# A four-layer convolution network on one NeuronCore: image b's depthwise taps in layer 3 move from TensorE to VectorE, and the order of taps, pieces and copies follows two clocks

## The chip, the cores and the metric

The program runs on one core of one Trainium2 chip. The metric is the device time of one execution in microseconds (us), the median of the runs shown. A separate profiled execution gives the span and the trace. Engines are named as in the profile: PE is TensorE's matmuls, PEld its weight loads, DVE is VectorE, ACT is ScalarE, POOL is GpSimd, SP is SyncE.

## The reference, cut to what matters

The input is x of shape (4, 48, 256, 256) in fp32. Each of four layers computes x + f(group_norm(x)). Layers 1 and 2 are recurrent scans over rows and columns and are not touched here. Layers 0 and 3 are gated depthwise networks:

```python
# layer 3 (HIDDEN = 144, C2 = 288); layer 0 is the same in another order with 96 / 192
y = einsum('oc,bchw->bohw', w_in, x)                 # 48 -> 288 channels
f = rfft2(y in 8x8 patches) * fft_mask; y = irfft2(f)
y = depthwise_conv3x3(y, w_dw)                       # 9 taps a channel
x1, x2 = split(y, 2, axis=1)
out = einsum('oc,bchw->bohw', w_out, gelu(x1) * x2)  # 144 -> 48
```

## The kernel before, in words

Layer 3 works on pairs of images, called a and b, and on strips of 8 rows: 2 pairs with 32 strips each and one short last step a pair (`tail`), so 64 full steps and 2 short ones. In a step 128 of the 144 channels of each half of each image fill one tile: `z_a0`, `z_a1`, `z_b0`, `z_b1` (half 0 feeds the Gelu, half 1 multiplies it). The last 16 channels of both halves and both images share the tile `z_m`. A step consists of these pieces, with the lines of the kernel before:

- `normed` (L904): four ACT instructions scale the raw strip into `u`. `turned` (L916): PE transposes `u`, ACT copies it to `xt`. `waves` (L930): PE transforms `xt`, ACT copies to `xf`.
- `spectrum` (L941): per column block q two PE matmuls into a PSUM tile `pz` and two DVE multiplications with the mask into `z`. Sixteen a step, two to a piece.
- `pixels` (L961): for each of the five groups 16 PE matmuls into `pp` and two ACT copies into `z_a0` and so on, after a copy of the two halo rows (by POOL for a and b, by ACT for m).
- `taps` (L988): the depthwise convolution on PE. A tap is a 32x32 diagonal matrix times a shifted window of 512 elements. Two generators, `lane(0)` and `lane(1)` (L1051), each own two of the four blocks of 32 channels; one turn of a lane issues one tap of one group, 8 matmuls. In a step each lane takes nine turns for each half of image a, then of b, and one of the two lanes nine for m. The results are held in PSUM tiles `pd`.
- `gate` (L1001): ACT takes the Gelu of half 0's `pd`, DVE multiplies it with half 1's into `g_a`, `g_b` or `g_m`.
- `mixed` (L1011): 40 PE matmuls of 32 rows by 64 columns into two PSUM tiles `po`, then eight DVE additions of the raw rows (`xo`) and the DMAs out on SP's queue.

All PSUM tiles of layer 3 come from one pool of four (L825[...])[...].

What sets the order: the whole program is unrolled while it is built. `in_turns` (L482) is the planner. In each round every lane takes one turn, which earns `pace` credit; pieces from the list `work` (L1070) are issued in their fixed order while the credit lasts or when no lane moved, if their condition (`free`, `full`) holds. Each piece carries a cost in the planner's us. Layer 0 has the same planner and similar pieces, for 64 strips. There the last 32 channels of both halves and images, `rests`, are already convolved on DVE by `unit` (L297), whose taps (L313) are handed out by `aside` (L515) according to a balance `ahead`; the main channels are convolved on PE (L278), and `mixed` (L340), `turned` (L367), `waves` (L381) and `back` (L399) follow. In layer 0 the program orders of PE and DVE are the order of issue (`manual_schedule`, L156); in layer 3 only PE's is (L826), and DVE, ACT, POOL and the queues are ordered by the framework. [...]

## Time and profile before

| | us |
|---|---|
| median of 3 runs (lowest, highest) | 14483.5 (14481.45, 14491.1) |
| the profiled execution, its own time | 14477.21 |
| its span in the profile | 14475.4 |
| PE busy in the span | 13474.0 |
| DVE busy | 5981.7 |
| ACT busy | 3295.6 |
| layer 0, from its first taps on PE to its last (264.72 to about 3230) | about 2965 |
| layer 3, from its first transposes to the end (9095.56 to 14475.4) | 5380 |

The span begins with some 230 us of statistics of the input, then comes layer 0, then layers 1 and 2 (to about 9090), then layer 3. A busy share is the time in which at least one instruction of the engine ran. fp32 matmuls appear twice in the records, so a tap's 8 matmuls are 16 records. The mean duration of one record does not say how fast records follow each other[...]; where a duration is needed, the distance from start to start in the timeline is the better one. One step of layer 3 is seen between two stores: the `xo` additions began at 9711.71 and, two steps later, at 9877.41, so a step took 82.9 us there.

### The profile page before, as it was taken

The numbers are of one execution on the slowest core, as the hardware profiler recorded it, in microseconds if no ns is written. First come the engines' busy times: TensorE is split into PE (matmuls) and PEld (weight loads), VectorE is DVE, ScalarE is ACT, GpSimd is POOL, SyncE is SP. The second block draws the span as 40 slices with busy tenths as digits, with TensorE's granted clock in tenths as the row PEclk, the third lists the DMA queues.
The fourth block names the chain that finished last, engine by engine and source line by source line (L and its number), as shares of the span: only waits on it lengthen the run. The fifth ranks groups of instructions, "written<-read, shape, count | busy, mean of one in ns | idle before, by whom it ended". The sixth has DMA issues, their size and how long they took to land.

```text
span 14475.4 us, 377862 instructions
## 1 busy us (share of the span) xinstructions
PE 13474.0 (93%) x175216; PEld 8571.1 (59%) x175216; DVE 5981.7 (41%) x10946; ACT 3295.6 (23%) x3108; POOL 1496.9 (10%) x1228
## 2 busy tenths in 40 slices
PE   2999999999998998899989988899999999999999
PEld 1444444446776775667767756566666666666666
DVE  6777777773333344533333445222222222222222
ACT  1333333332232000022320000222222222222222
POOL 0000010000000014400000144000000000000000
PEclk9999999999999998999999988999999999999999
DMA  7222222217756867677577676211111111111110
GB/s 166 53 49 53 54 51 51 54 41 146 145 144 162 152 132 190 160 156 145 145 167 151 135 190 156 31 20 24 21 20 24 20 20 20 24 20 20 24 20 18
DMA packets 1168867, 1221.55 MB, mean 84 GB/s; under 512 B 1025860, under 2 KB 1030460, under 8 KB 1106428
## 3 DMA queue, kind: packets, MB, share of 16 engines
q1 hardware_dynamic: 1069180, 649.60, 23.5%
q0 software_dynamic: 87488, 445.55, 11.0%
q10 hardware_dynamic: 10624, 102.24, 3.5%
q8 instruction: 1375, 22.53, 0.7%
q14 instruction: 200, 1.64, 0.0%
HBM read 699.82 MB, written 497.42 MB: 83 GB/s over the span
## 4 chain that ended last, share of the span: by engine, by line
PE 80%; DVE 8%; DMA 6%; issue 2%; ACT 1%; POOL 1%; SPq 1%; ACTq 0%; DVEq 0%; POOLq 0%
PE acc L598 33%; PE pd L994 20%; PE pp L977 8%; PE pd L278 4%; PE pz L946 4%; DVE acc L313 3%; DMA blk<-x 3%; PE po L1022 2%; PE pf L935 2%; PE ph L249 2%; DMA x<-blk 1%; PE pf L386 1%; DVE xo L419 1%; DMA gx<-in_x 1%; PE py L355 1%
## 5 line engine op out<-in xcount | busy, mean ns | idle before, releaser
L598 PE MATMUL acc<-line,w_down 96*96 96x256 f32 x12240 | 2649.9, 379 | 43.8 <-DMA in<-x 23.3
L598 PEld LDWEIGHTS acc<-line,w_down 96*96 96x96 f32 x12240 | 1995.6, 163 | 697.5 <-issue 44.6
L994 PE MATMUL pd<-z_b,diag 32*32 32x512 f32 x37152 | 1810.9, 596 | 10.5 <-DVE g_a L1009 10.5
L994 PE MATMUL pd<-z_a,diag 32*32 32x512 f32 x37152 | 1794.4, 596 | 0.1
L598 PE MATMUL acc<-line,w_left 96*96 96x256 f32 x6120 | 1360.8, 385 | 246.9 <-DVE line L781 246.9
L598 PE MATMUL acc<-line,w_right 96*96 96x256 f32 x6120 | 1336.9, 381 | 103.0 <-DVE line L742 39.1
L598 PEld LDWEIGHTS acc<-line,w_left 96*96 96x96 f32 x6120 | 1015.9, 166 | 591.5 <-DVE line L781 252.9
L278 PE MATMUL pd<-main,diag 32*32 32x512 f32 x36864 | 1337.7, 601 | 10.5 <-DVE g L292 5.4
L313 DVE SCALAR_TENSOR_TENSOR acc<-rest,wd,acc 128x1024 f32<-128x1024 f32 x1024 | 1313.7, 1324 | 72.5 <-ACT acc L307 70.6
L977 PEld LDWEIGHTS pp<-c_idft,z 128*128 128x128 f32 x10240 | 1156.8, 181 | 287.0 <-issue 265.3
L598 PEld LDWEIGHTS acc<-line,w_right 96*96 96x96 f32 x6120 | 1003.3, 164 | 436.6 <-DVE line L742 40.7
L977 PE MATMUL pp<-c_idft,z 128*128 128x128 f32 x10240 | 1223.8, 278 | 17.6 <-ACT z_b L981 17.6
L994 PEld LDWEIGHTS pd<-z_a,diag 32*32 32x32 f32 x37152 | 697.7, 103 | 508.1 <-issue 318.8
L948 DVE TENSOR_TENSOR z<-pz,mask 128x512 f32<-128x512 f32 x1024 | 701.5, 685 | 698.5 <-PE pz L946 698.5
L278 PEld LDWEIGHTS pd<-main,diag 32*32 32x32 f32 x36864 | 524.3, 103 | 681.6 <-issue 505.4
L994 PEld LDWEIGHTS pd<-z_b,diag 32*32 32x32 f32 x37152 | 619.0, 103 | 455.5 <-issue 278.6
L742 DVE SCALAR_TENSOR_TENSOR line<-acc,b_right,in 96x256 f32<-96x256 f32 x1020 | 489.4, 480 | 882.2 <-PE acc L598 836.8
L661 DVE TENSOR_TENSOR line<-acc,in 96x256 f32<-96x256 f32 x1020 | 429.1, 421 | 928.3 <-PE acc L598 900.2
L701 DVE SCALAR_TENSOR_TENSOR line<-acc,b_down,in 96x256 f32<-96x256 f32 x992 | 476.2, 480 | 808.5 <-PE acc L598 808.5
L791 POOL TENSOR_TENSOR blk<-blk,line 96x1024 f32<-96x1024 f32 x248 | 705.5, 2873 | 861.2 <-DVE line L781 447.4
L102 ACT ACTIVATE nrm<-nrm 96x2 f32<-96x2 f32 (+1 forms) x4 | 0.8, 204 | 3331.1 <-DVE nrm L101 3331.1
L1008 ACT ACTIVATE gl<-pd 128x1024 f32<-128x1024 f32 (+2 forms) x330 | 302.3, 926 | 1970.8 <-PE pd L994 1639.3
(147 smaller groups left out, 12161.3 us busy)
## 6 DMA issues: line engine op xcount, KB each, us to landing
blk<-x ACTq DMA_DIRECT2D x64, 1536.0 KB, 24.0
in<-x SPq DMA_DIRECT2D x248, 384.0 KB, 11.1
dn<-line POOLq DMA_DIRECT2D x124, 768.0 KB, 9.6
rt<-line POOLq DMA_DIRECT2D x124, 768.0 KB, 10.3
in<-rt SPq DMA_DIRECT2D x124, 768.0 KB, 7.3
in<-dn SPq DMA_DIRECT2D x120, 768.0 KB, 7.1
in<-up SPq DMA_DIRECT2D x240, 384.0 KB, 11.1
up<-blk POOLq DMA_DIRECT2D x56, 1536.0 KB, 24.0
```

The costliest lines, as they stand in the source:

```text
L278: nc.tensor.matmul(pd[32 * j : 32 * j + 32, i], diag[s, t, :], z[s, R2 * j + t // 3 : R2 * j + t // 3 + R2, t % 3 : t % 3 + W], start=(t = ...
L313: nc.vector.scalar_tensor_tensor(to, at(t, r), wd[:, 1, t : t + 1], to, ALU.mult, ALU.add)
L598: self.nc.tensor.matmul(acc, w[:, t, :], carry[:, :, t : t + m], start=(t == 0), stop=(t == 2))
L661: nc.vector.tensor_tensor(blocks(inner(line)), blocks(acc), xin[p][:, :, r % 2, :, r // 2, :], ALU.add)
L701: nc.vector.scalar_tensor_tensor(inner(line), acc, bd, new[p][r], ALU.add, ALU.add)
L742: nc.vector.scalar_tensor_tensor(blocks(inner(line)), blocks(acc), br, new, ALU.add, ALU.add)
L791: (nc.vector if w0 == 0 else nc.gpsimd).tensor_tensor(part, part, inner(ln[p][:, f::2])[..., lo:hi].rearrange("p w i h -> p i h w"), ALU.add)
L946: nc.tensor.matmul(pz[:, b, 0 : 2 * HD], xf[s, q, :], wi[s, :], start=True, stop=True)
L948: nc.vector.tensor_tensor(z[:, q, 0 : 2 * n].rearrange("p (b c) -> p b c", b=2), pz[:, :, 0:n], mask[:, :, 0:n].to_broadcast([128, 2, n]), ...
L977: nc.tensor.matmul(pp[0:n, q // 4, :, q % 4 * PW : (q % 4 + 1) * PW], z[:, q0 + q, k * NM : k * NM + n], self.idft, start=True, stop=True,)
L994: nc.tensor.matmul(pd[32 * j : 32 * j + 32, i, 0:n, :], diag[s, 2 if g == "m" else half, t, :], zt[g][s, R2 * j + t // 3 : R2 * j + t // 3 ...
L1008: nc.scalar.activation(gl[0:n, 0 : k1 - k0, 0:m], flat(x1), AF.Gelu)
```

## The change

In layer 3 image b leaves the lanes. `unit(step, half)` convolves `z_b0` or `z_b1` on DVE, as layer 0 does with its rest: ACT writes the first tap into a tile `acc0` or `acc1` (two instructions), and DVE adds the other eight taps in two pieces of four rows each, 16 `scalar_tensor_tensor` instructions for a half and 32 for a step. One ACT instruction takes the Gelu of `acc0` in place, and two DVE products join the halves. `mixed` reads the product with four matmuls of 128 rows by 64 columns (`wo_b`), and only image a keeps the small ones. `g_b` goes; `u` and `xf` now share one buffer (`tag="u"`, one buffer in `mid`). All halo copies are ACT's. DVE's program order in layer 3 is now the order of issue too.

The pieces of a step are put in another order: spectra of this step, `turned` of the next, group b0, `waves` of the next, m, a0, a1, b1, then the store of the step before.

The planner, in both layers, keeps two clocks, `self.pe` and `self.dve`. A turn of a lane adds 0.54 to the first, a piece its cost; pieces carry a second number, their DVE work, and those with such work wait until `self.dve < self.pe + 1.5`. Taps are handed to DVE while `self.dve <= self.pe + 1.0`. Conditions that depended on DVE's work (`until`, `full`) are compared with the PE clock.

The diff, cut to its core:

```diff
                             nc.vector.tensor_tensor(g[:, img, 0:2], state.pop((n, img)), pd, ALU.mult)
+                            self.after(self.pe + 1.0, 1.3)
...
-                last = [(3, 0.0, curve)] + [
-                    (2 - k, 1.28, lambda k=k: product(slice(64 - 64 * k, 128 - 64 * k))) for k in range(2)
+                last = [(0.3, 0.0, curve)] + [
+                    (2.2 - k, 1.28, lambda k=k: product(slice(64 - 64 * k, 128 - 64 * k))) for k in range(2)
...
-                return lambda: (n, 1) in ready, start, taps, last
+                return lambda: self.pe >= full.get(n, 1e9), start, taps, done, last
...
-                        yield always, 1.8, go, 1.2 * rest
+                                if rest:
+                                    full[n] = self.pe + 4.0
+                        yield always, 1.8, go, 1.3 * rest
...
-                            lambda: taken.get(n - 1, 0) == 6, 4.0, lambda: state.update(y=mixed(n - 1)),
+                            lambda: taken.get(n - 1, 0) == 6 and self.pe >= until[n - 1], 4.0,
+                            lambda: state.update(y=mixed(n - 1)), 0.0,
...
-            self.in_turns([lane(0), lane(1)], work(), 0.57, self.aside([unit(n) for n in range(len(strips))]))
...
+            self.in_turns([lane(0), lane(1)], work(), 0.57, [unit(n) for n in range(len(strips))])
...
+    def in_turns(self, lanes, pieces, pace, units):
...
+        self.pe, self.dve = 0.0, 0.0
+        side, going = self.aside(units), True
+        piece, credit, count, idle = next(pieces), 0.0, 0, 0
+        while lanes or piece or going:
+            moved = 0
...
-            spent += 0.54 * moved
+            self.pe += 0.54 * moved
             credit = min(credit + pace * moved, 2.0)
-            while piece and piece[0]() and (credit >= 0 or not moved):
+            while piece and (credit >= 0 or not moved) and piece[0]() and (not piece[3] or self.dve < self.pe + 1.5):
                 piece[2]()
-                credit = max(credit - piece[1], -5.0)
-                moved, spent = 1, spent + piece[1] - sum(piece[3:])
+                if piece[3]:
+                    self.after(self.pe + 1.0, piece[3])
+                self.pe += piece[1]
+                credit, moved = max(credit - piece[1], -5.0), 1
                 piece = next(pieces, None)
-            ahead, idle = max(min(ahead + spent, 2.5), -4.0), 0
-            while ahead > 0 or not moved:
-                cost = next(side, None)
+            got = True
+            while got:
+                got = next(side, None)
+                going = got is not None
+            idle = 0 if moved else idle + 1
+            self.pe += 0.0 if moved else 0.3
+            assert idle < 1000
...
+    def after(self, when, cost):
+        self.dve = max(self.dve, when) + cost
+    def aside(self, units):
+        later, begun = [], {}
+        def due():
+            while later and self.pe >= later[0][0]:
+                at, cost, work = later.pop(0)
                 if cost:
+                    self.dve = max(self.dve, at) + cost
                 work()
         def begin(k):
             if k < len(units) and k not in begun and units[k][0]():
+                begun[k] = self.pe + 3.0
                 units[k][1]()
+        for k, (_, _, taps, done, last) in enumerate(units):
             for i, (cost, tap) in enumerate(taps):
+                while k not in begun or self.dve > self.pe + 1.0 or self.pe < begun[k]:
+                    begin(k)
+                    due()
+                    yield False
                 if i >= len(taps) - 5:
                     begin(k + 1)
                 tap()
+                self.dve = max(self.dve, begun[k]) + cost
+                due()
+                yield True
+            done(self.dve)
+            at = self.dve
+            for wait, cost, work in last:
+                at += wait
+                later.append((at, cost, work))
         while later:
+            due()
+            yield False
...
-            st.enter_context(tc.manual_schedule(engines={mybir.EngineType.PE}))
+            st.enter_context(tc.manual_schedule(engines={mybir.EngineType.PE, mybir.EngineType.DVE}))
...
+            wo_b = wp.tile([128, 64], F32, name="wo_b")
+            nc.gpsimd.memset(wo_b, 0.0)
+            nc.sync.dma_start(wo_b[:, 0:C], self.a["L3_w_out"][0:NM, :])
...
-            gated = {g: wp.tile([128, 4, MM], F32, name=f"g_{g}", tag=f"g_{g}") for g in "ab"}
+            gated = {"a": wp.tile([128, 4, MM], F32, name="g_a", tag="g_a")}
...
-                u = mid.tile([112, NQ, 2, RB, PW // 2], F32, name="u")
+                u = mid.tile([112, NQ, 2, RB, PW // 2], F32, name="u", tag="u")
...
-                xf = mid.tile([112, NQ, 128], F32, name="xf")
+                xf = mid.tile([112, NQ, 128], F32, name="xf", tag="u")
...
                     nc.gpsimd.memset(t[:, 0:2, 1 : W + 1], 0.0)
-                elif g == "m":
+                else:
                     nc.scalar.copy(t[:, 0:2, 1 : W + 1], above[:, RB : RB + 2, 1 : W + 1])
-                else:
-                    nc.gpsimd.tensor_copy(t[:, 0:2, 1 : W + 1], above[:, RB : RB + 2, 1 : W + 1])
...
+                self.after(self.pe + 1.0, 0.1 + 0.6 * (k1 - k0))
+            whole, full, until = {}, {}, {}
+            def unit(step, half):
+                g, rows, made = f"b{half}", 1 if tail(step) else RB, []
+                parts = [(r, min(rows, r + RB // 2)) for r in range(0, rows, RB // 2)]
+                cost = [0.05 + 0.31 * (r1 - r) for r, r1 in parts]
+                at = lambda t, r, r1: zt[g][:, r + t // 3 : r1 + t // 3, t % 3 : t % 3 + W]
+                def start():
+                    acc = mid.tile([128, RB, W], F32, name=f"acc{half}", tag=f"acc{half}", bufs=2 - half)
+                    made.append(acc)
+                    for r, r1 in parts:
+                        nc.scalar.activation(
+                            acc[:, r:r1], at(0, r, r1), AF.Identity, bias=none, scale=wd[:, half, 0:1]
+                        )
+                def tap(t, r, r1):
+                    to = made[0][:, r:r1]
+                    nc.vector.scalar_tensor_tensor(
+                        to, at(t, r, r1), wd[:, half, t : t + 1], to, ALU.mult, ALU.add
+                    )
+                def done(when):
+                    taken[step, g] = 2
+                    until[step, g] = when
+                def curve():
+                    nc.scalar.activation(made[0][:, 0:rows], made[0][:, 0:rows], AF.Gelu)
+                    whole[step] = made
+                def product(r, r1):
+                    x1, x2 = whole[step][0], made[0]
+                    nc.vector.tensor_tensor(x1[:, r:r1], x1[:, r:r1], x2[:, r:r1], ALU.mult)
+                    if r1 == rows:
+                        full[step] = self.dve
+                taps = [(c, lambda t=t, rs=rs: tap(t, *rs)) for t in range(1, 9) for rs, c in zip(parts, cost)]
+                if half == 0:
+                    last = [(0.3, 0.0, curve)]
+                else:
+                    last = [(0.3, c, lambda rs=rs: product(*rs)) for rs, c in zip(parts, cost)]
+                return lambda: (step, g) in ready, start, taps, done, last
             def mixed(step):
                 h0 = s * RB - 1
                 js, n = (range(1), 1) if tail(step) else (range(4), R2)
                 pos = [ps_w.tile([128, 2, R2, W], F32, name="po", tag="w") for _ in js[::2]]
+                part = whole.pop(step)[0]
+                for j in js:
+                    nc.tensor.matmul(
+                        pos[j // 2][64:128, j % 2, 0:n, :], wo_b, part[:, R2 * j : R2 * j + n, :],
+                        start=True, stop=False,
+                    )
                 for i in range(5):
                     for j in js:
-                        for b in range(2):
+                        for b in range(2) if i == 4 else range(1):
                             r = slice(32 * j, 32 * j + 32)
-                            src = gated["m"][r, 0] if i == 4 else gated["ab"[b]][r, i]
+                            src = gated["m"][r, 0] if i == 4 else gated["a"][r, i]
                             nc.tensor.matmul(
                                 pos[j // 2][64 * b : 64 * b + 64, j % 2, 0:n, :], wo[r, i + b * (i == 4), :],
                                 src[:, 0 : n * W].rearrange("p (r w) -> p r w", w=W),
-                                start=(i == 0), stop=(i == 4),
+                                start=(b == 0 and i == 0), stop=(i == 4),
                             )
...
-                    for img in ("a", "b") + (("m",) if step[1] % 2 == l else ()):
+                    for img in ("a",) + (("m",) if step[1] % 2 == l else ()):
...
-                    free = lambda: last not in steps or k == 4 or taken.get((last, order[k]), 0) == 2
-                    return free, 0.0 if tail(step) else 3.8, go
+                    free = lambda: last not in steps or (
+                        taken.get((last, order[k]), 0) == (1 if k == 4 else 2)
+                        and self.pe >= until.get((last, order[k]), 0.0)
+                    )
+                    return free, 0.0 if tail(step) else 3.8, go, 0.0
...
                 def spectra():
                     for q in range(0, NQ, 2):
-                        yield always, 1.2, both(*[lambda q=q + i: spectrum(state["xf"], q) for i in range(2)])
+                        yield always, 1.2, both(*[lambda q=q + i: spectrum(state["xf"], q) for i in range(2)]), 2.0
                 def store(step):
-                    full = lambda: all(taken.get((step, g), 0) == (1 if g == "m" else 2) for g in order)
+                    done = lambda: self.pe >= full.get(step, 1e9) and all(
+                        taken.get((step, g), 0) == (1 if g == "m" else 2) for g in order
+                    )
                     def go():
                         mixed(step)
                         out.add(step)
-                    return full, 4.5, go
+                    return done, 8.2, go, 3.5
...
                 for n, step in enumerate(steps):
                     nxt = steps[n + 1] if n + 1 < len(steps) else None
                     ahead = nxt is not None and not tail(nxt)
                     later = steps[n + 2] if n + 2 < len(steps) else None
+                    if not tail(step):
+                        yield from spectra()
                     if ahead:
                         state["u"] = normed(nxt)
+                        turn, wave = front(nxt)
+                        yield turn
                     yield back(step, 2)
+                    if ahead:
+                        yield wave
+                    yield back(step, 4)
+                    yield back(step, 0)
+                    yield back(step, 1)
+                    yield back(step, 3)
                     if n:
                         yield store(steps[n - 1])
                     if later is not None and not tail(later):
                         fetch(later)
-                    yield back(step, 3)
-                    if ahead:
-                        yield from front(nxt)
-                    yield back(step, 4)
-                    if ahead:
-                        yield from spectra()
-                    if nxt is not None:
-                        yield back(nxt, 0)
-                        yield back(nxt, 1)
                 yield store(steps[-1])
-            self.in_turns([lane(0), lane(1)], work(), 0.6)
+            self.in_turns([lane(0), lane(1)], work(), 1.12, [unit(s, k) for s in steps for k in range(2)])
```

## The prediction, made before the result was known

> **What bounds the kernel now.** I read the slices of the page first, then the groups, then stage windows, and last the timeline of one step of layer 3 and one strip of layer 0.
>
> ```profile
> PE   2999999999998998899989988899999999999999
> DVE  6777777773333344533333445222222222222222
> PEclk9999999999999998999999988999999999999999
> ...
> L994 PE MATMUL pd<-z_b,diag 32*32 32x512 f32 x37152 | 1810.9, 596 | 10.5 <-DVE g_a L1009 10.5
> L313 DVE SCALAR_TENSOR_TENSOR acc<-rest,wd,acc 128x1024 f32<-128x1024 f32 x1024 | 1313.7, 1324 | 72.5 <-ACT acc L307 70.6
> L948 DVE TENSOR_TENSOR z<-pz,mask 128x512 f32<-128x512 f32 x1024 | 701.5, 685 | 698.5 <-PE pz L946 698.5
> ```
>
> The last fifteen slices are layer 3: PE is full and DVE stands at two tenths. The first nine are layer 0, where PE and DVE both work hard because DVE already convolves there. The windows of layer 0 and layer 3, then one step of layer 3 (columns: stretch, its length, busy time of PE, PEld, DVE, ACT, POOL, then the granted clock):
>
> ```profile
> 300.00:3200.00 2900.00, 2680.40 (x43290) 1198.30 (x43282) 2176.57 (x2983) 1049.22 (x992) 280.77 (x250) 0.96 0.21 51
> 9240.00:14440.00 5200.00, 5171.57 (x103242) 3194.35 (x103215) 1283.83 (x2798) 1358.41 (x1483) 159.53 (x264) 1.00 0.12 21
> ```
>
> ```profile
> 12001.44:12084.50 83.06, 82.83 (x1684) 51.86 (x1696) 20.62 (x45) 20.45 (x23) 1.99 (x4) 1.00 0.13 22
> ```
>
> Layer 3 has almost no idle PE time and the full clock; its length is the sum of PE's work. Layer 0 has 7.6% of idle PE time and a clock of 0.96, and it is the model of what layer 3 becomes. In its timeline PE waits for the gate's product ahead of `mixed`, and the clock of the next 5 us is halved:
>
> ```profile
> 1516.62 1.12 PE L348 MATMUL py<-gr,wo_r 64*128 64x512 f32 x2
> 1519.91 3.77 PE L348 MATMUL py<-gr,wo_r 64*128 64x512 f32 x6 [2.16 <-DVE g L292]
> ```
>
> ```profile
> 1520.00:1525.00 5.00, 5.00 (x22) 1.68 (x30) 3.45 (x3) 0.00 (x0) 0.00 (x0) 0.50 0.03 11
> ```
>
> [...]
>
> **The change, part by part, for one full step of layer 3.** Distances from start to start in the timeline of the step at 12001.44 are: one turn of both lanes 1.11 us (96 records, six turns, in 3.36); a `pp` piece 3.75; a `pz` piece 1.17; `pt` 1.7; `pf` 3.7; `po` 4.47. Before, a step has 81 turns of one lane, 40.5 double turns: 45.0. Pieces: 5 x 3.75 + 8 x 1.17 + 1.7 + 3.7 + 4.5 = 38.0. Sum 83.0, measured 83.06. So this sum can be trusted.
>
> *Removed from PE:* image b's 36 turns. Image a keeps 18 double turns, 20.0 us. The nine turns of m now have no partner, since the next a0 is not ready by then. A turn alone took 0.84 us (43 records in 2.26 us at 12053.59), so m costs 7.6 instead of 5.0. *Added to PE:* the store. Image a's 16 small matmuls run four at a time instead of eight: 8 rounds of 0.43 (rounds start at 12055.85, 12056.33, 12056.76) are 3.5, m's two rounds 0.9. Four `wo_b` matmuls of 128 rows and 512 columns: nearest is layer 0's `ph` of 112 rows, four records in 1.92 us, so eight records 3.8. The store is 8.2. *PE after:* 20.0 + 7.6 + 33.5 (the pieces without the store) + 8.2 = 69.3. Floor of the gain: 13.7 us a step, 64 steps, 877 us. The two short steps I take at zero (they may save some us).
>
> *DVE after:* four taps in a row took 4.86 us in layer 0, so 1.20 each: 32 are 38.4. Two products at 1.13: 2.3. Gates 2 x 1.13 + 0.6 = 2.9. Sixteen spectra at 0.74: 11.8. `xo` 2.7. Sum 58.1 (65.7 with the rows' mean durations, which overlap). Either is under 69.3: DVE alone doesn't bind. The planner books the same work at 66.7, and PE at 66.7. Its DVE clock is too slow by a seventh, so DVE will usually be early, and what counts is where one engine must wait for the other.
>
> *ACT after:* 20.5 now, plus four starts at 1.24 (5.0), a Gelu of 2048 elements (2.1, the time of `xn`), four halo copies at 0.62 (2.5), less two gates (2.0): 28. Hidden, unless something waits for one of these at once; that is priced below. POOL loses its copies, which bound nothing. SP's queue gets one small load of `wo_b` at the start; fetch and store DMAs move with their pieces, DMA share is 0.12, so zero.
>
> *Waits added on PE, none of them visible in the trace of before:*
> 1. a0's pixels are issued directly ahead of a0's taps, with no other lane running. ACT's second copy ends 1.1 us after the last `pp` (12084.32 plus 1.02 against 12084.24). Bounds 0 and 1.3, taken 1.2.
> 2. `u` and `xf` share a buffer. ACT can write `u` only when the last `pz` has read `xf`, and `turned` is the next piece. Four scalings last 2.93 us. Behind them on ACT stand the halo copy, the copies of b0 and the starts. Bounds 0 (if lane turns lie between) and 3.2, taken 3.0.
> 3. The store. The planner books DVE's `xo` one us after the store starts, but `po` is complete only at its end. So DVE stands some 6 us, with the gates of a (ready, but behind `xo`) and taps queued behind it. Two `po` and two `pd` then hold all four PSUM tiles, and PE's next `pz` waits for `xo` and gates: 2.7 + 2.3. Bounds 0 (if turns of a lie between) and 5.0, taken 1.5, since a lane's turns need no new tile until the half ends.
> 4. The clock after such waits. In the strip of layer 0 above `mixed` took 6.8 us without its wait where the same took 4.2 at the start of the layer (308.51 to 312.72). That is 2.6 for one. With one or two a step: bounds 0 and 5.0, taken 2.0.
>
> Sum of waits 7.7, so 77.0 us a step, 6.0 less than now, 64 x 6.0 = 384 us. Layer 0, of 46 us a strip, has a similar DVE share and spends about 3.5 us idle and some 3 us in a slow clock; the sum for layer 3 has the same size, which speaks for it.
>
> *Layer 0.* No work is added or removed; only the order changes. After `back` the old balance stands at -3.2 and the new clock at PE + 4.2; both let DVE have about two taps before the gate, so the 2.16 us wait ahead of `mixed` stays. Taken zero. Bounds: it vanishes with its slow clock in part (-2.0 a strip, -130 us), or pieces held for DVE's clock cost 1.5 a strip (+100).
>
> Against the profiled execution: 14477.2 - 384 = 14093. The median of the runs shown is 6.3 higher: 14100.
>
> **The rivals.** *A: nearly all of the gain arrives.* Lane turns or m lie in every gap and DVE, which is early, never holds PE. For it: PE's floor is 11 us over DVE's sum. Against it: wait 2 follows from a shared buffer, not from the order alone. Waits of 1.2 to 4.7 give 70.5 to 74.0 a step: 13,670 to 13,900. If layer 0's wait went as well, 13,550.
>
> *B: slower, because DVE's fixed order holds PE at each store.* DVE idles 6 us at `po`. The taps booked for that time come after it and stand ahead of the next spectra, whose `pz` tiles PE needs; and b1's pixels can't be written by ACT until b1's old taps are done, which blocks ACT's other copies. PE then waits about 5 to 7 us at the spectra besides 1.2 and 3.0, and spends three slow windows a step. 69.3 + 1.2 + 3.2 + 6 + 5 = 84.7, or 1.7 x 64 = 109 us slower: 14,590. It decides from 13.7 us of waits a step upward. For it: DVE's order was the framework's in layer 3 and is now fixed by a clock that is wrong by a seventh. Against it: layer 0, with the same kind of order, loses about 7 us of 46.
>
> *C: the planner's two clocks add so many idle steps that order alone matters little, and the gain is between.* 80 to 83 a step: 14,290 to 14,480.
>
> **How the numbers follow.** Forecast, 74 to 80 a step (13,900 to 14,290): 0.55. A: 0.22. B: 0.12. C: 0.11, of which 0.07 is faster and 0.04 within 0.2% (some 29 us, about what a measurement of this kernel can tell from no change). So faster 0.84, same 0.04, slower 0.12. The range 13,700 to 14,500 leaves out a small part of A and all of B.
>
> **What would show it.** A step distance between `xo` groups of 77 us; no `z_b` in the PE groups and 2048 more taps on DVE; PE around 90% busy in layer 3 with a clock of 0.95 to 0.98; a wait of `pt` for ACT's `u` of about 3 us a step; DVE waiting for `po` about 5 us. Layer 0 within 2 us a strip of before. It is wrong if PE stays at 98% (then A), or if PE waits for DVE's `z` or `xo` for more than 6 us a step (then B).

## The result, and the profile after

The changed kernel is slower: 14731.1 us (median of 4 runs, 14728.0 to 14740.5) beside 14487.3 us of the kernel before in the same session (4 runs, 14481.5 to 14497.4). The ratio is 1.0169, with a 95% interval of 1.0151 to 1.0186. The forecast was 14100, the range ended at 14500. The profiled execution has a span of 14738.7 us.

The page after, slices and groups that answer to those of before:

```profile
PE   2999999888999998899989986999999988999998
DVE  6777777663333344533333444666666666667667
PEclk9999999999999999899999998998898889989988
...
L1051 DVE SCALAR_TENSOR_TENSOR acc<-z_b,wd,acc 128x1024 f32<-128x1024 f32 (+1 forms) x2080 | 2490.5, 1266 | 23.3 <-ACT acc L1045 22.2
L1012 PE MATMUL pd<-z_a,diag 32*32 32x512 f32 x37152 | 1640.5, 680 | 288.7 <-ACT gl L1026 278.9
```

The taps of b have left PE, and 2080 taps appear on DVE. But PE in layer 3 isn't full any more, and its clock is at eight and nine tenths where it was at nine or above. The row of the remaining taps of a has a new entry, 278.9 us of waiting for ACT's Gelu. The stage windows (columns as before) say the same:

```profile
300.00:3200.00 2900.00, 2655.83 (x41495) 1152.26 (x41482) 2089.11 (x2859) 1029.31 (x960) 293.89 (x239) 0.93 0.20 50
9240.00:14440.00 5200.00, 4724.82 (x63614) 2774.01 (x63612) 3555.48 (x4662) 1748.35 (x1885) 4.07 (x10) 0.90 0.10 20
```

Both layers lost. Layer 3 begins at 9208.75 instead of 9095.56, so 113 us more lie ahead of it; 104 of them are layer 0's, whose last taps on PE begin at 3343.3 instead of 3239.0. From there to the end it is 5530 us instead of 5380, so layer 3 takes 150 us more. The sum, 263, is the whole difference of the spans. In the second window, layer 3's, PE is idle for 475 us, and a clock of 0.90 is worth some 520 of its 5200 us more, a small part of them while PE is idle.

One step of layer 3 between two stores, as a window, and two stretches in it with a slow clock, by which this document means a granted clock of 0.50:

```profile
12458.79:12543.48 84.69, 78.31 (x1060) 45.45 (x1063) 57.73 (x76) 28.79 (x31) 0.00 (x0) 0.90 0.10 20
12466.17:12479.82 13.65, 13.07 (x120) 4.58 (x120) 7.83 (x16) 1.44 (x2) 0.00 (x0) 0.50 0.12 12
12493.47:12496.88 3.41, 3.41 (x67) 1.24 (x66) 0.27 (x1) 1.32 (x2) 0.00 (x0) 0.50 0.02 5
```

DVE's 57.7 and ACT's 28.8 us are the forecast's 58.1 and 28. PE waits 6.4 us, and behind one wait it runs at half clock for 13.65 us, behind the other for 3.41, though it is busy. Half of that time, 8.5 us, is lost. The timeline of that step shows both waits on PE:

```profile
12461.99 1.24 PE L966 MATMUL pz<-wi,xf 48*128 48x288 f32 x8
12466.75 2.87 PE L1012 MATMUL pd<-z_a,diag 32*32 32x512 f32 x32 [3.52 <-ACT gl L1026]
...
12491.36 0.32 PE L941 MATMUL pt<-c_ident,u 112*128 112x112 f32 x1 [2.33 <-DVE acc L1051]
12492.07 1.78 PE L941 MATMUL pt<-c_ident,u 112*128 112x112 f32 x15 [0.39 <-ACT u L929]
```

ACT and DVE at the same time, each from its own timeline:

```profile
12465.15 0.62 ACT L988 COPY z_b<-z_b 128x512 f32<-128x512 f32 x1 [12.76 <-DVE acc L1051]
12465.67 1.93 ACT L1026 ACTIVATE gl<-pd 128x1024 f32<-128x1024 f32 x2
...
12489.08 2.93 ACT L929 ACTIVATE u<-raw,scp 112x512 f32<-112x512 f32 x4 [2.76 <-PE pz L966]
```

```profile
12458.79 2.74 DVE L1106 TENSOR_TENSOR xo<-po,raw 112x256 f32<-112x256 f32 x8 [11.64 <-PE po L1093]
12461.45 7.26 DVE L1051 SCALAR_TENSOR_TENSOR acc<-z_b,wd,acc 128x1024 f32<-128x1024 f32 x6
```

Read backwards, the first wait is a chain through the orders of two engines. PE needs `pd` free, so it waits for `gl`. The taps that `gl` reads had ended at 12462.06, and ACT had stood idle since 12452.39. But ahead of `gl` in ACT's order stands the halo copy of `z_b0` for the next step, which nobody needs before b0's pixels about 40 us later, and `gl` began at 12465.67, 0.52 us after the copy had begun. That copy overwrites two rows that taps on the old `z_b0` still read. It starts as the third of the six taps behind `xo` ends (at about 12465.1), and `xo` waits for the store's `po`: DVE stood 11.64 us. ACT's order here is the framework's; only PE's and DVE's are written by the kernel. The second wait is the buffer that `u` shares with `xf`: ACT starts `u` when the last spectrum has read `xf`, and `turned` is PE's next piece. (The row names DVE's tap as the releaser of 2.33; the four scalings of `u` that end one by one up to 12492.0 are what the first and second transposes read.)

**The theory** after this reading: the step is lost to short waits, each made by an instruction too early in its engine's order, and to the slow clock behind each (here 13.65 and 3.41 us at 0.50). **Rivals:** DVE's volume binds; the planner's wrong time scale is to blame; a wait removed is only replaced by another.

### The profile page after: what moved, and what is told of

The parts are those of the page before. It is cut to its first block, busy times and chain, and to the rows that moved or that the text cites. A ratio compares the mean times of both kernels' runs of the same rounds, so it can differ in the third digit from the quotient of the medians.

```text
span 14738.7 us, 300999 instructions
## 1 busy us (share of the span) xinstructions
PE 13219.7 (90%) x136516; PEld 8216.6 (56%) x136516; DVE 8435.0 (57%) x13024; ACT 3742.5 (25%) x3558; POOL 1364.7 (9%) x974
## 4 chain that ended last, share of the span: by engine, by line
PE 77%; DVE 11%; DMA 6%; ACT 3%; issue 1%; SPq 1%; POOL 1%; ACTq 0%; DVEq 0%; POOLq 0%
PE acc L613 33%; PE pd L1012 12%; PE pp L995 8%; PE pd L278 6%; PE pz L966 4%; DVE acc L1051 3%; DVE acc L314 3%; DMA blk<-x 3%; PE po L1093 2%; PE ph L249 2%; PE ph L257 2%; PE po L1084 2%; PE pf L955 1%; PE pf L390 1%; ACT u L929 1%; PE pt L941 1%
## 5 line engine op out<-in xcount | busy, mean ns | idle before, releaser
L1051 DVE SCALAR_TENSOR_TENSOR acc<-z_b,wd,acc 128x1024 f32<-128x1024 f32 (+1 forms) x2080 | 2490.5, 1266 | 23.3 <-ACT acc L1045 22.2
L1012 PE MATMUL pd<-z_a,diag 32*32 32x512 f32 x37152 | 1640.5, 680 | 288.7 <-ACT gl L1026 278.9
L278 PE MATMUL pd<-main,diag 32*32 32x512 f32 x36864 | 1422.2, 629 | 45.7 <-DVE g L292 37.5
L314 DVE SCALAR_TENSOR_TENSOR acc<-rest,wd,acc 128x1024 f32<-128x1024 f32 x1024 | 1279.2, 1301 | 0.0
L995 PEld LDWEIGHTS pp<-c_idft,z 128*128 128x128 f32 (+1 forms) x10240 | 1165.1, 182 | 202.5 <-issue 166.1
L995 PE MATMUL pp<-c_idft,z 128*128 128x128 f32 (+1 forms) x10240 | 1224.3, 279 | 13.7 <-ACT z_a L999 13.7
L1012 PEld LDWEIGHTS pd<-z_a,diag 32*32 32x32 f32 x37152 | 460.9, 109 | 956.2 <-issue 457.5
L796 DVE SCALAR_TENSOR_TENSOR line<-acc,b_left,in 96x256 f32<-96x256 f32 x992 | 475.7, 480 | 531.2 <-PE acc L613 531.2
L966 PE MATMUL pz<-wi,xf 48*128 48x288 f32 x4096 | 765.0, 500 | 12.5 <-DVE z L972 8.7
```

The lines of the kernel that those rows point to most:

```text
L278: nc.tensor.matmul(pd[32 * j : 32 * j + 32, i], diag[s, t, :], z[s, R2 * j + t // 3 : R2 * j + t // 3 + R2, t % 3 : t % 3 + W], start=(t = ...
L314: nc.vector.scalar_tensor_tensor(to, at(t, r), wd[:, 1, t : t + 1], to, ALU.mult, ALU.add)
L796: nc.vector.scalar_tensor_tensor(inner(line), acc, bl, new[p][r], ALU.add, ALU.add)
L966: nc.tensor.matmul(pz[:, b, 0 : 2 * HD], xf[s, q, :], wi[s, :], start=True, stop=True)
L995: nc.tensor.matmul(pp[0:n, q // 4, :, q % 4 * PW : (q % 4 + 1) * PW], z[:, q0 + q, k * NM : k * NM + n], self.idft, start=True, stop=True,)
L1012: nc.tensor.matmul(pd[32 * j : 32 * j + 32, i, 0:n, :], diag[s, 2 if g == "m" else half, t, :], zt[g][s, R2 * j + t // 3 : R2 * j + t // 3 ...
```

## The experiments

In the table, the last column has PE's largest item, summed from 9300 us to the end. All ratios are to the kernel before, run in the same session.

| run | median us | ratio (95%) | largest wait of PE in layer 3, us in all |
|---|---|---|---|
| the change | 14731.1 | 1.0169 (1.0151–1.0186) | taps of a for `gl`, 279 |
| e1_l0_old | 14637.9 | 1.0104 (1.0089–1.0119) | the same, 272 |
| e2_halo_pool | 14548.5 | 1.0042 (1.0026–1.0059) | `pz` for `z`, 257 |
| e3_late_add | 14660.0 | 1.0119 (1.0104–1.0134) | `po` for `z_b`, 277 |
| e4_turn_later | 14348.7 | 0.9903 (0.9888–0.9917) | taps of a for `gl`, 185 |
| e5_few_taps | 14457.0 | one run | `pt` for `u`, 155 |
| e6_turn_dvehalo | 14248.1 | 0.9830 (0.9816–0.9845) | `pz` for `z`, 256 |
| e7_turn_lateadd | 14102.3 | 0.9728 (0.9712–0.9744) | `po` for `z_b`, 248 |
| e8_measured_clock | 14405.7 | 0.9938 (0.9923–0.9953) | taps of a for `z`, 290 |
| e9_all_three | 13741.8 | 0.9485 (0.9471–0.9499) | `po` for b's product, 24 (two waits) |
| e10_no_turn | 14039.3 | 0.9694 (0.9678–0.9711) | `pt` for `u` (two rows), 160 |
| e11_all_new_l0 | 13837.4 | 0.9551 (0.9538–0.9564) | not used |
| e12_l0_room | 13796.2 | 0.9521 (0.9508–0.9534) | not used |

**e1: layer 0 with the planner of before,** layer 3 as changed (`in_turns3` is the new planner under another name).

```diff
-            self.in_turns([lane(0), lane(1)], work(), 0.57, [unit(n) for n in range(len(strips))])
+            self.in_turns([lane(0), lane(1)], work(), 0.57, self.aside([unit(n) for n in range(len(strips))]))
```

> Layer 0 gets back its old planner, layer 3 stays as changed. The profile of the change says that layer 0 lost 135 us (2966 to 3100) and layer 3 lost 150. If the two clocks are what costs layer 0 its time, this run takes about 14,600 us, with layer 0 at 2966 again and its clock at 0.96. If layer 0 is slower for another reason than its planner, it stays near 14,730.

It came out 93 us below the change, and its layer 3 lasts the same 5530 us. So the new order alone costs layer 0 about 93 us, which the prediction had at zero, and layer 3's loss is its own.

**e2: the halo copies of a and b by POOL again.**

```diff
-                    nc.scalar.copy(t[:, 0:2, 1 : W + 1], above[:, RB : RB + 2, 1 : W + 1])
+                    nc.gpsimd.tensor_copy(t[:, 0:2, 1 : W + 1], above[:, RB : RB + 2, 1 : W + 1])
```

> In layer 3 the halo rows of a and b are copied by POOL again, as before; nothing else changes. Theory one (ACT's queue): after each store the Gelu of image a stands on ACT behind the halo copy of z_b, which waits for DVE's last tap; PE waits 3.5 us for the PSUM tile and then runs 13.7 us at half clock. Without it some 3.5 + 6.8 = 10 us a step vanish, up to 640 us: about 14,150 us, a step near 75. Theory two (DVE's backlog): the six taps behind the blocked xo additions hold the pz tiles anyway, so PE's wait only changes its name, to DVE's z: 14,600 to 14,740.

183 us came back, which lies between the two expectations. So the halo copies on ACT cost something, but the wait got another name: with ACT free (25 us of waits for `gl` are left), PE ran on to the next spectra and there waited for DVE, which was behind `xo`.

```profile
PE pz L966 <- DVE z L972: 256.5, 57, 4.5
PE pt L941 <- DVE acc L1053: 137.3, 59, 2.3
```

**e3: the additions `xo` issued after the store's time,** so that taps stand ahead of them on DVE.

```diff
-                    return done, 8.2, go, 3.5
+                    yield done, 8.2, go, 0.0
+                    yield always, 0.0, lambda: added(step, *state["po"]), 3.5
```

> The xo additions of a store are handed to DVE after the store's matmuls have passed on the PE clock, so that the taps of that time stand ahead of them. Theory two (DVE's order): DVE's idle time at po falls from about 10 us a step to under 4, the taps end sooner, and a step gets 4 to 6 us shorter: about 14,400 us. Theory one (only ACT's queue matters) also gains, since z_b's last tap is done sooner, but less: 14,550. If DVE's idle time at po is slack, no change or slower, 14,730, because the po tiles are held longer.

71 us came back, less than either theory expected. The wait behind the store went, and one of nearly the same size appeared ahead of it: the store's `po` for ACT, whose pixel copies into `z_b1` were queued behind the same early halo copy of `z_b0` (it starts at 12496.19, ACT having stood 8.23 us).

**e4: `turned` moved behind b0's pixels, `waves` behind m's.** This takes the reason of the wait for `u` away by giving ACT other PE work to hide its scalings.

```diff
-                        yield turn
                     yield back(step, 2)
                     if ahead:
-                        yield wave
+                        yield turn
                     yield back(step, 4)
+                    if ahead:
+                        yield wave
```

> The turned piece is moved behind the pixels of b0, and waves behind those of m, so that ACT's writing of u (2.9 us) lies under a pixel piece. If the shared buffer of u and xf costs its wait (2.7 us) and the half clock behind it (3.4 us, that is 1.7 lost), a step gets 4.4 us shorter: about 14,450 us. If the wait only moves, to waves or to a0's first taps, 14,650 to 14,740.

This one move is worth 382 us, more than expected, and makes the kernel faster than before. The wait of `pt` is gone. 382 over 60 full waits is 6.4 us each, though the wait itself was 2.7: the rest is clock, and a smaller wait at `gl` (185 instead of 279), less a new one of `pz` for `z` (49).

**e5: seven of every eight taps of b left out.**

```diff
-                taps = [(c, lambda t=t, rs=rs: tap(t, *rs)) for t in range(1, 9) for rs, c in zip(parts, cost)]
+                taps = [(c, lambda t=t, rs=rs: tap(t, *rs)) for t in range(1, 2) for rs, c in zip(parts, cost)]
```

> Of the changed kernel's eight taps on DVE only one is left in layer 3 (28 of 32 DVE tap instructions a step are left out, so image b's convolution is incomplete). PE's list is nearly the same. If PE's own work is 69.3 us a step, as summed, and the rest of the 85 us comes from waiting for DVE and the slow clock behind it, a step takes 69 to 75 us (the wait for u stays), about 14,050 to 14,150 us in all with the new layer 0. If PE's work was summed too small, the step stays above 78 us: 14,350 or more.

One step of e5, between two stores:

```profile
12399.65:12481.57 81.92, 77.37 (x1049) 43.18 (x1049) 25.33 (x49) 28.78 (x32) 0.00 (x0) 0.92 0.11 21
```

DVE now works 25 us of a step, and the step is still 81.9 us long, with a clock of 0.92. With more than half of DVE's work gone, this step is 2.8 us shorter (4.3 on average, 274 us over 64 steps, in a single run). DVE's volume doesn't bind. The length is that of the expectation's second branch, but PE's work was not summed too small (e9 below): PE still waits in each step, for `u` (155 us in all), `gl` (71) and `z` (43), with the slow clock behind.

**e6 and e7: combinations,** both with layer 0's old planner and e4's move. e6 adds image b's halo copies on DVE, e7 the late additions instead.

```diff
+                elif g[0] == "b":
+                    nc.vector.tensor_copy(t[:, 0:2, 1 : W + 1], above[:, RB : RB + 2, 1 : W + 1])
```

> Layer 0 with its old planner, turned behind b0's pixels, and the halo rows of b copied by DVE itself (two copies a step), so that ACT no longer waits for DVE's last tap. If ACT's queue is what holds PE after a store, its 3.5 us and the slow clock behind them go: 14,250 (the two earlier edits) less 200 to 400, 13,900 to 14,050 us. If DVE's backlog of taps behind xo holds the pz tiles in any case, 14,200 to 14,250, with PE waiting for DVE's z.

> Layer 0 with its old planner, turned behind b0's pixels, and xo's additions handed to DVE after the taps of the store's time. Here the backlog behind xo is gone but the halo copy of b stays on ACT. If the backlog is the cause, the spectra run without a wait and a step is some 3 to 6 us shorter than with the two edits alone (14,250): 13,900 to 14,050. If DVE is late at b1's pixels then, as it was with the late additions alone (4.4 us a step of waiting ahead of the store), it stays at 14,150 to 14,250.

e4 with layer 0's 93 us off would stand at about 14255. Against that e6 gains 7 us, no more than repeated runs of one kernel differ, and e7 153. In e6, as its rival expected, PE waits for DVE's spectra, which stand behind `xo` and taps; in e7 there is one wait a step, ahead of the store, and ACT's timeline names the same halo copy. First e6, then e7, PE and ACT:

```profile
12070.24 2.29 PE L1031 MATMUL pz<-wi,xf 48*128 48x288 f32 x8 [4.54 <-DVE z L1037]
```

```profile
12033.05 5.34 PE L1151 MATMUL po<-acc,wo_b 128*64 128x512 f32 x8 [3.64 <-ACT z_b L1066]
```

```profile
12031.45 0.62 ACT L1055 COPY z_b<-z_b 128x512 f32<-128x512 f32 x1 [8.10 <-DVE acc L1118]
```

**e8: e6 with layer 3's planner costs set to durations measured** (a turn of two lanes 1.1, of one 0.86; a tap 1.2; a spectra piece 1.5 of DVE; a gate 1.1, booked to start earlier). The main line of the edit:

```diff
-            self.pe += 0.54 * moved
+            self.pe += (0.0, 0.86, 1.1)[moved]
```

> As the run with DVE's halo copies, but in layer 3 the two clocks are given measured durations: 1.2 us for a tap piece, 1.5 for a pair of spectra, 1.1 for a gate, 0.86 for a turn of one lane alone and 1.1 for both. If a DVE clock that is a seventh slow and a PE clock that books a lone turn at 0.54 are what puts DVE's instructions at the wrong places, the waits shrink by half or more: 13,850 to 14,000 us. If what counts is which instruction stands ahead of which at the store, not the clocks' scale, it equals the run without (within 50 us).

It is 158 us slower than e6, which neither side expected, with PE waiting for `z` again: six taps still stand between `xo` and the first spectrum. A truer clock doesn't cure the queues; that rival falls for this order of pieces and this one setting.

**e9 and e10: all three edits together** (DVE's halo copies, late additions, later turns; layer 0's old planner), and the same without the later turns.

> Layer 0 by the planner of before; in layer 3 as in the changed kernel, but with three edits together: image b's halo copies by VectorE, the turns of u moved behind b0's pixels (waves behind m's first turns), and the xo additions handed to VectorE after the store's pieces, so that taps stand ahead of them. Theory (three short waits a step, each made by an in-order queue, and the slow clock after each, took the gain): the 3.64 us wait of e7_turn_lateadd at the store, made by the z_b copy on ScalarE, is gone with 3.4 us of half clock, so at least 5.3 us a step less than e7: 13,650 to 13,800 us, TensorE waiting under 1 us a step. Rival (the waits move elsewhere: VectorE, with 58 + 1 us and the additions late, now holds b0's pixels or the store itself): 14,050 or more, with a new wait of TensorE on VectorE of 3 us or more in each step.

> As e9_all_three, but with the turns of u left where the change has them, straight behind the ACTs that make u. It prices the buffer that u shares with xf. Theory: the wait of turned on u (2.3 to 2.8 us) comes back with 3.4 us or more of half clock behind it: 4 to 6 us a step, so 250 to 380 us above e9_all_three. Rival (the u wait is only a filler for slack that something else would take): within 60 us of e9_all_three.

Both came out as the theory said. e9 is 5.2% faster than the kernel before, and in its steps PE is full at full clock. Two steps of e9, from the first matmul of a store to that of the second store after it, and one step of e10:

```profile
12132.50:12273.94 141.44, 140.80 (x2102) 85.95 (x2097) 118.59 (x159) 54.66 (x59) 0.00 (x0) 1.00 0.13 24
```

```profile
12026.97:12102.05 75.08, 72.09 (x1060) 44.30 (x1063) 59.47 (x79) 27.64 (x29) 0.00 (x0) 0.98 0.11 23
```

```profile
12051.77:12055.18 3.41, 3.41 (x31) 2.74 (x46) 0.31 (x1) 1.47 (x2) 0.00 (x0) 0.50 0.03 5
```

A step of e9 is 70.7 us. DVE has as much to do in it as in the change (59.3 us, two halo copies included), and 14 us a step are gone. The e10 step is 4.4 longer than e9's: 2.7 us of the wait for `u`, and 1.7 of slow clock, the 3.41 us at half speed in the last line. Taken from e9, e7 and e6 price the other edits: without DVE's halo copies +360 us, without the late additions +506, without the later turns +298. Ahead of the late additions the halo edit was worth 7 us (e6 against e4). The two edits at the store take away two queues that hold PE near the same store, so each is worth far less until the other is made. That a wait removed is only replaced held for each of them alone, not for both.

**e11 and e12: layer 0.** e11 is e9 with the new planner in layer 0. e12 hands out layer 0's taps, and only those, 1.5 us of the planner's time later:

```diff
-                while k not in begun or self.dve > self.pe + 1.0 or self.pe < begun[k]:
+                while k not in begun or self.dve > self.pe - 0.5 or self.pe < begun[k]:
```

> Layer 0 as in the changed kernel, layer 3 as in e9_all_three. Theory (the two layers' losses are independent, and the new planner costs layer 0 what e1_l0_old gave back): 85 to 105 us above e9_all_three, 13,825 to 13,850 us. Rival (the layers share something, or the 93 us of e1 came in part from elsewhere): less than 50 or more than 150 us above it.

> As e11_all_new_l0, but in layer 0 a tap is handed to DVE only while its clock is at least 0.5 us behind PE's (the change: until it is 1.0 us ahead of PE's); layer 3 keeps 1.0. Theory (in layer 0 the gate's product stands behind taps that were handed out up to 1.0 + 1.28 us too early, which is the wait of 2.07 us of TensorE for g): that wait falls under 1 us and layer 0 gains 1 to 2 us a strip, 60 to 130 us below e11. Rival (ACT's order is what counts: its Gelu of the unit stands ahead of its copies for the next pieces and waits for the last taps, which now come later still): no gain or a loss, e12 from 20 below to 150 above e11, with TensorE's waits on ACT grown.

e11 is 95.5 us above e9, as expected: the two layers' losses add up. In the strip of layer 0 shown here, of the change, the gate's product `g` stands behind six taps on DVE, and PE waits for it:

```profile
1568.55 7.61 DVE L314 SCALAR_TENSOR_TENSOR acc<-rest,wd,acc 128x1024 f32<-128x1024 f32 x6
1576.09 1.21 DVE L292 TENSOR_TENSOR g<-gl,pd 128x1024 f32<-128x1024 f32 x1
```

```profile
1577.35 1.75 PE L278 MATMUL pd<-main,diag 32*32 32x512 f32 x16 [2.07 <-DVE g L292]
```

Waits of PE in layer 0 (300 to 3200), first the kernel before, then the change, then e12:

```profile
PE py L348 <- DVE g L292: 124.8, 61, 2.3
PE pt L372 <- ACT gl L289: 79.3, 51, 2.0
```

```profile
PE ph L249 <- ACT yt L380: 93.1, 23, 4.7
PE py L352 <- DVE g L292: 45.1, 49, 1.0
PE pd L278 <- DVE g L292: 37.5, 17, 2.7
```

```profile
PE py L352 <- DVE gr L330: 112.5, 57, 2.5
```

Waiting for `g` is not what is new: in all rows it was 132 us before and 112 in the change. New is the first row of the change, `ph` for `yt`, and in the strip looked at it is layer 3's mechanism again. ACT's copy `yt`, which takes the tile `pt` out of PSUM, stands behind the Gelu of the unit, and that waits for taps on DVE:

```profile
3184.09 1.05 ACT L324 ACTIVATE gr<-acc 64x1024 f32<-64x1024 f32 x1 [4.49 <-DVE acc L314]
3186.25 1.68 ACT L380 COPY yt<-pt 128x896 f32<-128x896 f32 x2
```

```profile
3187.18 3.78 PE L249 MATMUL ph<-xn,wi 48*128 48x512 f32 x8 [4.56 <-ACT yt L380]
```

PE's idle time in this stretch grew by only 25 us, from 220 to 244. Its clock fell from 0.96 to 0.93, which is some 87 us of the 2900, so the larger part of layer 0's loss is clock.

e12 gained 41 us, less than the 60 expected and more than the rival's 20. All waits for `g` and nearly all for `yt` went, against the rival's forecast of more waits on ACT, but the unit's own product `gr`, which stands behind the later taps, now comes 2 us late at `mixed`. So the hand-out of taps decides which of two consumers waits. What each wait of layer 0 costs in clock stays open.

What was not tried: separate buffers for `u` and `xf` (whether both fit beside the new tiles is not shown); e4's move tests the same wait in another way. A written order for ACT wasn't tried either; e7 and e9 show only that moving the copy off ACT is enough.

## Why the prediction was wrong, by its own steps

The terms of its sum for a step, with what they measured. e9's step is 70.7 us with PE busy at full clock, including the wait for a0's pixels.

| term | taken (bounds) | measured |
|---|---|---|
| PE's work | 69.3 | 69.6: e9's 70.7 less the 1.15 of the next row |
| wait 1, a0's pixels | 1.2 (0–1.3) | 1.15: 96 records of taps behind them take 4.56 us, elsewhere 3.41 |
| wait 2, `u` shares with `xf` | 3.0 (0–3.2) | 2.72: 2.33 + 0.39 |
| wait 3, at the store | 1.5 (0–5) | 3.52 |
| slow clock | 2.0 (0–5) | 7.7: what is left of 84.7 (by the granted clock 8.5, in part under waits) |
| a step | 77.0 | 84.7 |

The account of the slow clock below needs one more line of the kernel before, PE's next work after the `mixed` that the prediction prices:

```profile
1526.76 2.35 PE L278 MATMUL pd<-main,diag 32*32 32x512 f32 x64
```

- **PE's, DVE's and ACT's sums** were right, and so was "DVE alone doesn't bind" (e5). The gain that they promise exists: e9 has it.
- **The slow clock was the step that failed most.** It was sized from one wait of layer 0, 2.6 us, as "one or two a step", and both its value and its upper bound were too small. The 2.6 itself is a misreading: the 6.8 us of `mixed` count from 1519.91, after the wait, and leave out its first two matmuls. From 1516.62 to the next taps at 1526.76, less the wait, it is 8.0 against 4.2, so 3.8 for one wait. Then 2.0 was taken, less than the price of one, in a step for which the text itself lists three waits. In the step shown 13.65 us at half clock cost 6.8 us after one wait, and 3.41 us cost 1.7 after the other. The length of a wait did not set its price: 3.52 us cost 6.8 here, and e7's 3.64 us cost 1.7.
- **Wait 3 was right in place and wrong in mechanism.** The text had PE wait for `xo` and the gates on DVE, and took lane turns as cover. The gates did stand behind something, but on ACT: "Hidden, unless something waits for one of these at once" was said of ACT's added work, the four halo copies among it, and these were not followed along ACT's queue. That an instruction that stands holds those behind it was assumed; in the change ACT stood 12.76 us at the copy, and `gl`, ready for the last 3.1 us of them, came after it. Where a copy is moved to another engine, what it waits for is moved too; this one carried DVE's backlog into the Gelu's queue (e2, e7, e9).
- **Layer 0, "taken zero", was wrong** by 93 us in the paired runs (e1) and 104 in the profiles, about its upper bound of 100. The argument that both rules let DVE have two taps before the gate didn't hold: in the strip shown six stood there. And the wait that grew was another, on ACT.
- **Rival B** had the right sign and, at 84.7 us, even the step's length, but that match is luck. Its chain of taps behind a late `xo` and ahead of the spectra is what e2, e6 and e8 show; in the change itself PE was held before that, by the Gelu behind b0's halo copy. Its other chain, b1's pixels waiting for b1's own taps, was not seen: in e3 and e7 b1's pixels were late, but behind b0's halo copy. Half of the step's loss over e9 was clock. With 64 × 1.7 = 109 us it was short by layer 0 and by 41 us of layer 3 that this one step doesn't show. What spoke against it, that layer 0 "loses about 7 us of 46", was itself read too high: the text's own window gives 3.5 idle and, at 0.96, 1.8 in clock. The likeness didn't carry over either: in layer 0 POOL copies the halo rows, so none stands ahead of a Gelu on ACT.
- **Of the signs it named,** the taps' rows, PE around 90% busy (4724.8 of 5200), the `pt` wait of about 3 us and layer 0 within 2 us a strip (104 / 64 = 1.6) came true. The step of 77 us did not, nor the clock of 0.95 to 0.98 (0.90), nor DVE's 5 us at `po` (10.5 to 11.6). Neither sign of being wrong came: PE waited for ACT, not for DVE's `z` or `xo`.

## What to carry to other kernels

When work moves to another engine, follow every instruction that moves with it, copies of 0.6 us too: write down what it waits for and what stands behind it (here ACT stood 12.76 us at such a copy, with PE's `gl` behind it). A wait on TensorE should be priced with the slow clock behind it, here 0 to 11.9 us for waits of 2.1 to 3.6. Curing one of two queues at the same place can gain much less than curing both: the halo edit was worth 7 us alone and 360 with the late additions made. Where PE is the bound, put a piece that needs nothing new between a producer on ACT and its consumer on PE (e4: 382 us for a change of order).

## What the runs showed of the hardware

How long the half clock lasted differed widely behind waits of like length: 3.41 us behind e7's wait of 3.64 us and e10's of 2.72, 6.83 us (from 1577.65) behind the change's wait of 2.07 in layer 0 shown above, 13.65 behind the 3.52 of the change, 23.89 (from 9628.98) in a step of e3 behind 2.72. Half of each, 1.7, 3.4, 6.8 and 11.9 us, is what it cost. Behind another wait of 2.07 us for `g` in the change's layer 0 the clock stayed at 1.00 (1530.95 to 1534.50), so that wait cost nothing more. In e7 matmuls of 128 rows came first:

```profile
12033.34:12036.75 3.41, 3.41 (x5) 0.91 (x4) 2.86 (x3) 3.38 (x4) 0.00 (x0) 0.50 0.00 0
```

In the change the alternation of a turn of both lanes and a spectra piece stayed at 0.50 for 13.65 us, though the same alternation right after ran at 1.00 (12480.00 to 12488.90). In that step of e3 (with 15.90 us too the steps at 9971.84, 10309.76 and 10647.68, each four steps on) the turns of m, one lane alone and without a pause, took 15.90 us where they took 8.17 at 9724.64 in the next step, and the clock stood at 0.50 throughout:

```profile
9633.93 15.90 PE L1014 MATMUL pd<-z_m,diag 32*32 32x512 f32 x144
```

```profile
9634.00:9649.80 15.80, 15.80 (x161) 7.53 (x144) 4.74 (x4) 1.91 (x1) 0.00 (x0) 0.50 0.01 2
```

In the change's step the same 144 records took 8.12 us at 1.00 (12497.22 to 12505.34). So the same steady work ran at either clock. No run here varied only what PE executes behind a wait, so the reason stays open.

POOL's copy of `z_b` in e2 took 7.0 us on average and that of `z_a` 0.62, the same shape; before, both took 0.62. In e2 the first runs while DVE convolves. Its end follows DVE: all 126 records of it over 1 us end 0.48 us after DVE has ended one of b's taps (72) or products (54), as here:

```profile
12051.37 1.52 POOL L990 COPY z_b<-z_b 128x512 f32<-128x512 f32 x1 [9.83 <-DVE acc L1053]
```

```profile
12045.16 7.26 DVE L1053 SCALAR_TENSOR_TENSOR acc<-z_b,wd,acc 128x1024 f32<-128x1024 f32 x6
```

So the record looks like a wait for DVE with some 0.5 us of copying at its end, not like slow work; no run varied this alone.
